# A written-out order of work, searched anew for the first stretch of a four-layer residual chain

## The chip, the cores and the metric

The kernel runs on one core of a Trainium2 chip. The metric is device time in microseconds (us) of one execution, as the median of the runs. Five engines take part, each with its own queue of instructions that it works off strictly in order: TensorE (PE, with its weight loads shown apart as PEld), VectorE (DVE), ScalarE (ACT), GpSimd (POOL) and SyncE (SP), which here does nothing but start DMA transfers. POOL starts the indirect gathers. An instruction that has to wait for another engine holds up all that stand behind it on its own engine.

## The reference

The input x has 128 sequences of 64 tokens with 256 features. Four layers are added to it one after the other, each steered by conditions of the sequence:

```python
x = x + _L0_cond_ref(x, cond_512, ...)   # modulated linear -> attention over 16 heads per token -> modulated linear
x = x + _L1_cond_ref(x, cond_512, ...)   # down and up projection with weights made per sequence, relu, residual
x = x + _L2_cond_ref(x, ids..., ...)     # layer norms with gathered gains, six terms joined, two-layer net, layer norm
x = x + _L3_cond_ref(x, cond_512, ...)   # per sequence: U = (mu @ W_dec + b_dec); out = x @ (U V) + bias
```

In layer 0 the weight is scaled by a style and a demodulation of each sequence (`style = s @ aff_w.T + aff_b`, `demod = rsqrt(sum((w*style)**2) + eps)`), and queries, keys and values are the same projection, so that the heads of one token attend to one another. Layer 1 makes `w_down = down_project * dg + db` and `w_up = up_project * ug + ub` for each sequence. Layer 2 gathers gains and offsets by token ids and adds three conditions, each of which is a small net with a layer norm of its own (`mem`, `noi`, `res`). Layer 3 makes a matrix of rank 30 for each sequence from `W_dec`.

## The kernel before, in words

The 8192 tokens are worked on in 16 blocks of 512 tokens (8 sequences). A prologue, called block -1, makes what depends on the sequences alone:

- `prologue_keys`: style and demodulation of layer 0. `style` (product on PE by `product`, L629, addition on DVE, L725), `square` on POOL (L734, L735), `root` (DVE L742, ACT L743), the copy of the demodulation of block 0 (`dmk`, ACT L767).
- `prologue_rest`: the products for layer 1 (`down_gb`, `up_gamma`, `up_beta`; copies on ACT at L790 and L795, stores to DRAM by SP at L791 and L799), the scaled weights of layer 2 (ACT L819, POOL L824 and L825), and U of layer 3. For U, 16 loads of `W_dec` (`wd`, SP L842) feed 16 groups of products (PE L851); the first eight results are moved by DVE (L866), the others by ACT (L858), and U goes to DRAM (SP L881). Then tables by rows (`by_row`, ACT L658 and L676, DVE L662 and L687, the copy ACT L901), and the three small nets (PE L629, DVE L931, ACT L937, DVE L940, DVE L958, POOL L619 and L621, DVE L964, PE L976, ACT L982, DVE L1002).

Each block then runs through `attention` and `rest`:

- loads: `xT` (SP L1039), `ids` (L1044), `dmk` (L1052), `gdb` (L1062), `wup` and `ubb` (L1073), `uT` (L1084); POOL makes `xsT` (L1097), gathers `pw` (L1112) and makes the weights of layer 1 from `gdb` (`wdn`, L1129 and L1135) and from `wup` and `ubb` (L1142, L1143).
- two pairs of attention: keys (PE L1191, DVE L1202, POOL L1213), transposes (DVE L1228, L1245), `kR` (ACT L1237), `v` (PE L1256, ACT L1261), scores (PE L1276, 128 small matmuls), their maxima (DVE L1289, ACT L1302, PE L1311, ACT L1321, DVE L1328 and L1337), the subtraction of the maxima (PE L1350), exponentials (ACT L1364, twice a pair), weighted values (PE L1381, 128 small matmuls), then DVE L1394, L1402, POOL L1405 (`att`), PE L1418, DVE L1425; after both pairs the output projection (PE L1155, DVE L1162 and L1173).
- layers 1 to 3: PE L1573, ACT L1582, PE L1591, DVE L1604, PE L1648, ACT L1655, layer norms, the eight products L1738 per half, and so on to the output store.

PSUM is shared out as four buffers `bank` and one `sc`; scores and exponentials have only the one `sc`, `kR`, `kT`, `xsT` and `gdb` exist once, `wdn` and `wup` twice. Such a buffer is a slot: who takes it next waits for its last user.

What sets the order is written out by hand: `TURNS` holds, for the prologue and each block, one number for each operation. An operation's number is `max(blk, 0) * TURN + tables[blk][k]`, and `Plan.order` emits, of all operations whose inputs are emitted and for which a slot is free, the one with the lowest number. The instructions of an engine stand in the order of emission, and the slots are given out in that order too. Blocks overlap: while block 0 is in `rest`, blocks 1 and 2 are in `attention`. `spin` is an unread product: a matmul of zeros into a `bank` that nobody reads (PE L638). Their count follows from the table of block -1:

```python
SPINS = len(TURNS[-1].split()) if -1 in TURNS else 331
...
    while plan.noted[-1] + 1 < SPINS:
        spin()
    done = plan.order()
```

## Time and profile before

| | |
|---|---|
| runs | 839.22, 828.07, 828.92, 830.99 us; median 829.96 us |
| the profiled execution | 827.48 us, of which span 825.6 us |
| granted TensorE clock, mean | 0.974 |
| VectorE, ScalarE, GpSimd | busy 588.0, 361.3, 565.2 us |
| PE busy by stretches of 10 us, 0 to 130 us | 6.33, 8.95, 7.42, 7.12, 8.85, 6.82, 5.25, 7.50, 9.09, 7.57, 8.85, 9.10, 7.83 |
| granted clock in the same stretches | 0.89, 0.93, 1.00, 1.00, 0.83, 1.00, 0.63, 0.84, 0.85, 0.83, 1.00, 1.00, 1.00 |
| DMA share in the same stretches | 0.75, 0.86, 0.62, 0.81, 0.99, 0.67, 0.90, 0.39, 0.67, 0.72, 0.44, 0.40, 0.38 |

Times in the trace count from the first instruction. "Idle before" is the time for which an engine had nothing running ahead of an instruction, with what ended it; "issue" means that nothing the profile shows held the engine. The clock is the share of full speed that PE was granted. The DMA share is the mean busy share of the core's 16 DMA engines. Queue q1 carries SP's transfers, q0 the gathers, and the queues called "instruction" carry the engines' own instructions.

### The profile page before, as it was taken

What the parts mean: (1) busy time and instruction counts of PE and PEld (TensorE: products, weight loads), DVE (VectorE), ACT (ScalarE), POOL (GpSimd) and SP (SyncE); (2) the same over time, 40 slices, a digit from 0 to 9 for tenths busy, and PEclk for the clock granted to TensorE, in tenths of its full rate; (3) what the DMA queues carried; (4) which work ended last, traced back from release to release, by engine and by line L of the source; (5) the groups of instructions that cost most, each with busy time, mean ns of one, the idle gap of its engine ahead of it and who ended that gap; (6) DMA issues with size and microseconds to landing.
All of it is one profiled execution on the core that took longest, in us unless ns stands there. A gap on an engine that the chain in (4) does not pass through costs nothing.

```text
span 825.6 us, 29444 instructions
## 1 busy us (share of the span) xinstructions
PE 755.5 (92%) x12843; PEld 489.9 (59%) x12843; DVE 588.0 (71%) x1320; ACT 361.3 (44%) x664; POOL 565.2 (68%) x544
## 2 busy tenths in 40 slices
PE   7777889999999999999999999999999989998695
PEld 5655665665666565666666666656566565654353
DVE  4646796966868686969687786869695967765435
ACT  1564335442536362544435353636254343434331
POOL 5453879394877878586869688786789485818243
PEclk9996999999999999999999999999999999999888
DMA  8786643234342234343333333342434231022001
GB/s 271 243 244 189 206 135 81 77 104 105 95 126 70 84 96 129 92 116 94 105 103 94 117 96 102 97 120 68 129 92 117 73 89 51 11 58 81 35 1 52
DMA packets 59297, 87.63 MB, mean 106 GB/s; under 512 B 6456, under 2 KB 42400, under 8 KB 59168
## 3 DMA queue, kind: packets, MB, share of 16 engines
q1 hardware_dynamic: 54048, 68.96, 28.4%
q0 software_dynamic: 5120, 16.78, 7.2%
q8 instruction: 101, 1.65, 0.9%
q14 instruction: 28, 0.23, 0.1%
HBM read 72.48 MB, written 13.24 MB: 104 GB/s over the span
## 4 chain that ended last, share of the span: by engine, by line
PE 62%; DVE 20%; issue 5%; ACT 4%; POOL 4%; DMA 3%; SPq 0%; another core or an unknown queue 0%; DVEq 0%; POOLq 0%; ACTq 0%
PE bank L1738 26%; PE bank L1785 5%; PE bank L1191 5%; PE sc L1276 4%; DVE st L611 4%; DVE mr L1289 3%; PE bank L1688 3%; PE bank L1381 2%; PE bank L1573 2%; PE bank L1155 2%; PE bank L629 2%; DVE bank L1162 2%; ACT e L1364 1%; PE bank L1648 1%; PE bank L1823 1%
## 5 line engine op out<-in xcount | busy, mean ns | idle before, releaser
L1289 DVE TENSOR_REDUCE mr<-sc 128x16 f32<-128x1024 f32 x64 | 75.7, 1210 | 16.1 <-PE sc L1276 16.1
L1364 ACT ACTIVATE e<-sc 128x1024 f32<-128x1024 f32 x64 | 62.4, 1027 | 34.3 <-PE sc L1350 34.2
L1112 POOL DMA_INDIRECT pw<-in_pw,idx x64 | 65.3, 1021 | 15.9 <-issue 8.2
L1155 PE MATMUL bank<-osT,wo 128*128 128x512 f32 x128 | 62.2, 614 | 5.2 <-DVE osT L1425 5.1
L1276 PEld LDWEIGHTS sc<-kR,kT 20*64 20x64 f32 x4096 | 48.8, 134 | 24.8 <-issue 10.9
L1738 PE MATMUL bank<-uu,w_s 128*128 128x512 f32 x128 | 63.3, 598 | 0.0
L1191 PE MATMUL bank<-wk,xsT 128*128 128x256 f32 x256 | 62.3, 386 | 1.0 <-DVE uu L866 0.6
L1738 PE MATMUL bank<-uu,w_h 128*128 128x512 f32 x128 | 62.8, 613 | 0.0
L1276 PE MATMUL sc<-kR,kT 20*64 20x64 f32 x4096 | 54.3, 236 | 8.7 <-issue 5.9
L1237 ACT ACTIVATE kR<-kT,early 128x1024 f32<-128x1024 f32 x32 | 39.7, 1241 | 51.5 <-DVE kT L1228 51.5
L1738 PE MATMUL bank<-uu,w_t 128*128 128x512 f32 x128 | 61.3, 605 | 0.2 <-ACT uu L1655 0.2
L1738 PE MATMUL bank<-x2T,w_x 128*128 128x512 f32 x128 | 60.0, 593 | 0.0
L1381 PEld LDWEIGHTS bank<-e,v 64*32 64x32 f32 x4096 | 44.3, 106 | 24.1 <-issue 20.1
L1785 PE MATMUL bank<-w,uu 128*128 128x256 f32 x240 | 55.9, 386 | 2.3 <-DVE uu L1758 2.3
L1191 PEld LDWEIGHTS bank<-wk,xsT 128*128 128x128 f32 x256 | 48.5, 196 | 12.8 <-issue 3.5
L1381 PE MATMUL bank<-e,v 64*32 64x64 f32 x4096 | 50.7, 228 | 5.5 <-issue 5.5
L1693 ACT COPY uu<-bank 128x512 f32<-128x512 f32 x64 | 36.4, 587 | 38.1 <-PE bank L1688 36.5
L1202 DVE TENSOR_TENSOR kxe<-bank,dmk 128x512 f32<-128x512 f32 x32 | 22.0, 688 | 43.5 <-PE bank L1191 38.2
L1129 POOL TENSOR_TENSOR wdn<-gdb,late 128x512 f32<-128x512 f32 x32 | 40.6, 1284 | 15.8 <-PE bank L1573 15.2
L1785 PEld LDWEIGHTS bank<-w,uu 128*128 128x128 f32 x240 | 44.4, 190 | 9.8 <-DVE uu L1758 4.1
L1228 DVE STREAM_TRANSPOSE kT<-kxe 128x512 f32<-128x512 f32 x64 | 42.1, 684 | 9.3 <-POOL kxe L1213 9.3
L1213 POOL TENSOR_TENSOR kxe<-kxe,kbr 128x512 f32<-128x512 f32 x32 | 40.7, 1273 | 10.3 <-DVE kxe L1202 10.1
(241 smaller groups left out, 1782.6 us busy)
## 6 DMA issues: line engine op xcount, KB each, us to landing
xT<-in_xT SPq DMA_DIRECT2D x32, 256.0 KB
gdb<-dgdb SPq DMA_DIRECT2D x16, 512.0 KB
ubb<-ugub SPq DMA_DIRECT2D x32, 256.0 KB
wup<-ugub SPq DMA_DIRECT2D x32, 256.0 KB
ids<-in_ids SPq DMA_DIRECT2D x16, 256.0 KB
ud<-uu SPq DMA_DIRECT2D x8, 512.0 KB
uT<-ud SPq DMA_DIRECT2D x16, 256.0 KB
dmk<-demod_k SPq DMA_DIRECT2D x60, 64.0 KB
```

The source lines that it names most:

```text
L1112: lambda tl=tl, n=n: nc.gpsimd.indirect_dma_start(out=pw[tl // 2].t[:, tl % 2, :], out_offset=None, in_=a["pw"], in_offset=bass.IndirectOf ...
L1129: lambda w=w, dp=dp: nc.gpsimd.tensor_tensor(w(), gdb.t[:, :, 0:64], dp, ALU.mult),
L1155: nc.tensor.matmul(ps.t, owT[:, c, bass.ts(oc, 128)], osT.t[:, c, :], start=(c == 0), stop=(c == C - 1))
L1191: nc.tensor.matmul(ps.t[:, bass.ts(l, F)], xsT.t[:, c, mine2].rearrange("p (n l) -> p l n", l=2)[:, l, :], kwT[:, c, :], start=(c == 0), s ...
L1213: lambda: nc.gpsimd.tensor_tensor(kxe.t[:, :, :, 0:D], kxe.t[:, :, :, 0:D], heads(kinds["kbr"][0]).unsqueeze(1).to_broadcast([128, 2, H, D ...
L1228: lambda l=l: nc.vector.transpose(kT.t[:, l, :].rearrange("p (g h t) -> p h g t", h=H, t=QT), kxe.t[:, l, :, :]),
L1276: nc.tensor.matmul(sc.t[64 * c : 64 * c + 64, q, bass.ts(tg, 64)], cut(kT.t)[r, tg // 4, c, tg % 4, :], cut(kR.t)[r, tg // 4, c, tg % 4, : ...
L1289: lambda two=two: nc.vector.tensor_reduce(mr.t[:, two, :], sc.t[:, two, :].rearrange("p q (g n) -> p q g n", g=TG), AX.X, ALU.max),
L1364: lambda k=k: nc.scalar.activation(es[k].t, sc.t[:, 2 * k : 2 * k + 2, :], AF.Exp, scale=0.25),
L1381: nc.tensor.matmul(placed(pr[c].t)[32 * q : 32 * q + 32, l, g, :, :], v.t[r, l, :].rearrange("p (g q d) -> p g q d", g=4, q=4)[:, g, q, :] ...
L1738: lambda ps=ps, w=w, src=src, fc=fc, c=c, n=n: nc.tensor.matmul(ps.t, w.t[:, c, bass.ts(fc, 128)], src.t[:, c, :], start=(n == 0 and c == ...
L1785: nc.tensor.matmul(ps.t[:, bass.ts(l, F)], s2.t[:, c, bass.ts(2 * p + l, 128)], w2.t[:, c, :], start=(c == 0), stop=(c == C - 1),)
```

## The change

Only numbers in `TURNS` change: 200 of the entries for the prologue (which grow from 254 to 260, so that there are 29 unread products rather than 23), 160 of 184 for block 0 and 186 of 188 for block 1. No operation, shape or tile is altered. The tables of blocks 2 to 15 stay.

```diff
 TURNS = {
     -1: """
-    -652225 -652207 -501809 -501797 549383 103302 97834 98988 -85347 -290328 36942 -280951 36928 -327022 -327038
...
-    15405911 16048186 16073369 -309973 14522440 16005249
+    -652225 -652207 -501809 79623 549383 100856 97834 98988 -135716 -290328 -135684 -290340 -135703 -327038 -327044
...
     """,
     0: """
-    -484581 84372 -652203 -35682 684863 1289506 1005368 578863 1258365 2419509 2111364 2061858 1597541 357479
...
+    -484581 84372 -652203 -135703 684863 1289506 1005368 1030611 944977 2419509 2111364 2063037 1598720 357479
...
     """,
     1: """
-    -394079 -394092 -482733 -425615 -297831 -337865 -325537 -299039 -482716 297196 735637 407985 -421370 1532404
...
+    -475790 -480517 -480506 -439237 -295604 -295623 -306545 -306564 -481411 409304 726230 398578 374496 1282148
...
     """,
```

The numbers mean something only through the order that follows from them. On each engine that order is the old one but for moves over a few places, all within about the first 220 us. Those of the first 110 us that pass more than a neighbour, or pass one of another kind:

| engine | what moves |
|---|---|
| SP | load of `idx` behind `w2` and the first half of block 0's `xT` |
| SP | both halves of block 1's `xT` ahead of a `wd`, `down_gb` and `up_gamma` |
| SP | the four `dmk` loads of block 1 ahead of the store L791 |
| SP | second `ubb` load of block 0 ahead of two `wd`, `int_b1` and `mem_W1` |
| SP | `ids` and `gdb` of block 2 ahead of the `wup` loads of block 1 |
| PE | second `dmk` product (L629) ahead of a style product and of the first keys of block 0 (L1191) |
| PE | first keys of block 1 (L1191) behind the second scores of block 0 (L1276) |
| PE | of the two `wd` products (L851) after that, the later one first |
| PE | L1311 of block 0's second pair ahead of a `wd` product (L851) |
| PE | second transposes of block 0 (L1648) ahead of block 1's second L1381 |
| ACT | `v` of block 0 (L1261) ahead of `kR` (L1237) and three others |
| ACT | L1302 of block 0's second pair ahead of an L858 and an L819; the three L819 still ahead of L1321 |
| ACT | `kR` of block 1 (L1237) and an L858 ahead of the exponentials of block 0's second pair (L1364) |
| ACT | L1655 of block 0 ahead of two L982 |
| DVE | maxima (L1289) of block 0's second pair ahead of block 1's L1202; of block 1's first pair ahead of two L1228 |
| POOL | `xsT` of block 1 (two L1097) behind L1213 and a gather of block 0 |
| POOL | L1142 of block 1 behind two L1129 of block 2 and the L1143 of block 0 that follows them |

Of the unread products seven stand at the start as before, one moves from 119 us to ahead of the first L1311 near 33 us, two are put in near 150 to 160 us and two near 655 us, near 725 us there are two fewer, and at the end of the last block four more.

## The prediction

> **What bounds the kernel now.** I read the page first (busy times, slices), then the chain of waits, then the PE timeline of the first 130 us, because the change orders only what runs there. The page says that TensorE (PE) is the bound, and where it is not:
>
> ```profile
> PE 755.5 (92%) x12843; PEld 489.9 (59%) x12843; DVE 588.0 (71%) x1320; ACT 361.3 (44%) x664; POOL 565.2 (68%) x544
> ...
> PE   7777889999999999999999999999999989998695
> ...
> q8 instruction: 101, 1.65, 0.9%
> ```
>
> A slice is 20.6 us: PE is at 7 to 8 tenths in the first six and at 9 after that. By stretches of 10 us it is busy 100.7 of the first 130 us and 42.74 of the 44 us from 200 to 244. What this change can win or lose lies in those 29 us; later delays pass to the end, since PE has no slack to take them up. The largest pieces, from the PE timeline (start, duration, line, what it writes and reads, count, idle time before and who ended it):
>
> ```profile
> 37.31 1.90 PE L1191 MATMUL bank<-wk,xsT 128*128 128x256 f32 x8
> 40.30 1.59 PE L1276 MATMUL sc<-kR,kT 20*64 20x64 f32 x128 [1.09 <-ACT kR L1237]
> ...
> 45.88 1.62 PE L1381 MATMUL bank<-e,v 64*32 64x64 f32 x128
> ...
> 50.48 0.66 PE L1418 MATMUL bank<-ident,att 128*128 128x128 f32 x4 [1.33 <-POOL att L1405]
> ...
> 56.38 1.42 PE L1381 MATMUL bank<-e,v 64*32 64x64 f32 x121
> 61.31 0.31 PE L1381 MATMUL bank<-e,v 64*32 64x64 f32 x7 [3.51 <-issue]
> 61.55 0.49 PE L629 MATMUL bank<-early,p 128*128 128x128 f32 x2
> 61.97 1.92 PE L1276 MATMUL sc<-kR,kT 20*64 20x64 f32 x119
> 67.33 0.49 PE L1276 MATMUL sc<-kR,kT 20*64 20x64 f32 x9 [3.44 <-issue]
> 67.75 1.12 PE L1256 MATMUL bank<-ident,kV 128*128 128x128 f32 x4
> ```
>
> Two stops of 3.51 and 3.44 us stand inside a run of equal matmuls, with nothing that PE waits for ("issue"). Between them lie 7+2+119 = 128 matmuls, with their weight loads 256 instructions; queue q8 moved 1.65 MB in 101 packets, 16.3 KB each. So these are instruction blocks that came late. Stretches of 1 us show why (PE, PEld, DVE, ACT, POOL busy, clock, DMA share, GB/s):
>
> ```profile
> 57.00:58.00 1.00, 0.80 (x84) 0.65 (x66) 0.23 (x1) 0.74 (x4) 0.83 (x1) 1.00 0.68 242
> 58.00:59.00 1.00, 0.00 (x0) 0.00 (x0) 0.53 (x2) 0.77 (x2) 0.00 (x0) 1.00 0.20 67
> 59.00:60.00 1.00, 0.00 (x0) 0.00 (x0) 0.57 (x2) 0.89 (x4) 0.00 (x0) 1.00 0.00 0
> ...
> 64.00:65.00 1.00, 0.00 (x0) 0.00 (x0) 0.37 (x2) 0.85 (x2) 0.00 (x0) 0.50 1.17 241
> ```
>
> In the trace's packets q8's block starts at 58.92, when the last data packet is through, takes 0.97 us, and PE goes on at 61.31, 2.4 us after the start. The next block starts at 64.52, 3.2 us after the resumption, amid a burst of loads, and PE goes on 2.8 us later. After the stops the granted clock is 0.50 from 62.5 to 72.7.
>
> [...]
>
> **The change part by part.** I read the new order out of the tables by the rule of `order()`: the lowest number among operations whose inputs and slots are ready. PE's sequence changes little: the same 7 early unread products, then swaps of neighbours. The order of each engine is the old one from about 220 us on, and so are nearly all slots' predecessors. Both late block boundaries stay where they were, one matmul earlier in L1381 and in L1276. So the fetches are not removed; what moves is when PE and the DMA queue reach them.
>
> (1) *Start, to 31 us.* On SP xT of block 1 goes ahead of a `wd`, `down_gb` and `up_gamma`; it no longer stands behind the `wd` slot wait at 18.73 and issues near 14.6. On PE L629 for the second half of `dmk` goes ahead of the keys; the keys come 1.1 us later, behind ACT L767. Cover: DVE's L1245 at 20.67 waits on the `wd` landing at 18.76 and L866 anyway. The two `demod_o` products swap while DVE keeps its order: the scores come 0.3 late, taken up by the 0.62 us fetch stop at 26.80. I take 0; without cover +1.1.
>
> (2) *Keys of block 1 behind the second scores.* L1191 at 37.31 now runs after L1276, so PE idles from 37.4 to 40.3 (L1276 still waits for ACT L1237, behind both exps), and the 1.90 us fall into a stretch with no gap until 49.15. One unread product ahead of L1311 adds 0.22 (119.03 to 119.25, start to start). L1381 at 45.88 comes 2.1 later.
>
> (3) *ACT.* PE now feeds the two `wd` products (L851, 42.68) in reversed order while ACT takes the old first one first: its L858 starts at 48.0 rather than 44.63. Behind it: 1.26, the copies L1302 0.49, the other L858 1.26, three L819 at 0.72: L1321 at 53.1 rather than 49.37. Behind that, L1237 (1.24) and an L858 (1.26) now precede the exps: 57.0 rather than 53.31. L1381 (56.38) starts near 59.8, +3.5, and would reach the block's end at 61.2.
>
> (4) *The first fetch.* It ran when the DMA queue was empty. SP's issues before it hang on L799, which waits for ACT L795 behind PE's L629 at 41.83 (now +1.9), and on freed `wd` slots: I shift them 1.0 to 1.5, so the fetch starts at 60.2 and PE resumes at 62.6: +1.3; 2.2 of the 3.5 fall into time lost anyway. Bounds: 0 (queue unmoved) and +3.5 (moves with the work).
>
> (5) *The second fetch.* PE reaches it 2.58 after the resumption, at 65.2. The burst that delayed it is released by ACT L901, 59.44 before and 61.6 now. Asked ahead of the burst, the block starts 1.3 after the resumption (as it did at 28.74 after the stop that ended at 27.42) and PE goes on at 66.7; in it, 3.2 and 68.6. I take 67.6: +0.3 against 67.33; with both ends of (4), -1.9 to +2.2.
>
> (6) *Clock.* In the half-clock stretch L1256 takes 1.12 (0.66 elsewhere), L1418 1.06 (0.66), twelve L851 2.77 (1.59 by 1.06 for eight): 2.0 lost. Shorter stops may free a third of it: -0.7 (0 to -2.0; above 0 if the gap of (2) halves the clock too).
>
> [...]
>
> (7) *POOL.* L1142 of block 1 ran at 71.44, inside an idle time of 10.61 us ahead of L1129. It now follows L1143 at 85.77, ahead of L1097 (88.42), att and ry, which the chain of waits runs through: +1.25 (0 to 1.27).
>
> (8) *ACT's L1655 ahead of two L982.* PE's L629 at 95.66 waited 1.43 for the bank that DVE L1202 frees; it now gets the bank of L1655, free by 93.6. The next gate is L982, 95.07: -1.0. DVE is full from 110 to 120 (9.25 of 10), so half stays: -0.5 (0 to -1.9).
>
> (9) *Six more unread products*, 0.22 each where PE is full: +0.5 (0 to 1.3). Swaps among neighbours elsewhere: 0, bounds -0.7 to +0.7 (one DVE row of 0.68).
>
> Sum of (5), which contains (2) to (4), and (6) to (9): +0.3-0.7+1.25-0.5+0.5 = +0.85 on the profiled execution's 827.48 us (span 825.6): 828.3. The runs are 828.07, 828.92, 830.99 and 839.22, median 829.96; the lower three average 829.3. I forecast **830.0 us: no difference**.
>
> **Rivals.** *Slower by over 1%:* the loads move with the work, so both stops remain whole behind the 3.5 us of (3); the gap of (2) halves the clock for two more stretches of 3.4 us (1.7 each); (7) and (9) are paid, (8) is not: 3.5+3.4+1.3+1.3 = +9.5, 838 to 839. It decides from where the first late block starts after 61.5. For: every link is a wait in the profile. Against: most of SP's issues there wait for nothing. *Faster by over 1%:* both blocks are asked for in a free queue: -3.5-3.4-2.0 = -8.9, 821. Against: PE has only 2.58 us between the boundaries, and even the free case costs 1.3+2.8. *Smaller gain:* the second block precedes the burst and the clock stays whole: about -4, 826. *Smaller loss:* (4) at its upper end: +5, 834. *The change does not do what it says:* later-asked fetches cost the same, the rest cancels; this lies inside the forecast.
>
> **How the numbers follow.** A measurement of this kernel can tell about 1%, 8.3 us. Chances: forecast (827 to 832.5) 0.45, smaller loss 0.23, smaller gain 0.17, slower by over 1% 0.11, faster by over 1% 0.04. Leaving out a tenth on either side: 823 to 838.
>
> **What would show it.** Right: the stops in L1381 and L1276 still there, the first under 2 us and ended near 62.6; PE idle over 2.5 us before L1276 at 40; L1142 between L1143 and L1135 near 87; L629 with no wait near 95. Wrong: a first stop of 3 us or more, new "issue" stops of over 1 us, or half-clock stretches after 100 us that before does not have.

## The result and the profile after

The changed kernel is slower, by less than one per cent. Before has a median of 832.89 us (69 runs, 823.59 to 843.12), after of 837.62 us (43 runs, 830.92 to 845.05); the ratio is **1.0070 [1.0054, 1.0086]**, that is about 5.8 us. Runs over 1.5% above the fastest of their kernel are left out of all ratios and of the means and differences below. The forecast was no difference, 830.0 us, on a median of before of 829.96 (its first four runs). The 837.62 us lie inside the range of 823 to 838 and within the 1% that was set as the bound, but the kernel did move, and the rival that came nearest was the "smaller loss" (834), for another reason than the one given for it.

The profiled execution of after took 838.04 us (span 836.3, mean clock 0.968), that of before 827.48 (825.6, 0.974). They lie 10.6 us apart and the kernels 5.8: each profile is one draw from its kernel's spread. Which of the 10.6 us belong to the change had to be found by runs.

From the page of after (busy times; the span in 40 slices of 20.9 us; the instruction queue):

```profile
PE 763.6 (91%) x12849; PEld 494.4 (59%) x12849; DVE 592.2 (71%) x1320; ACT 361.1 (43%) x664; POOL 566.2 (68%) x544
...
PE   7677888999999999999999999999999979998696
...
PEclk8989999999999999999999999999999989999888
...
q8 instruction: 101, 1.65, 0.9%
```

The picture is that of before: 7 to 8 tenths in the first slices, 9 after that, the same 1.65 MB of instructions in 101 packets. Three things differ. The second PE slice has 6 tenths. The clock is lower in the first slice and in the third (42 to 63 us), and higher in the fourth (63 to 84 us; 9 tenths, 6 in before). The slice from 669 to 690 us has 7 tenths and a lower clock.

The PE timeline of after for the stretch that the prediction worked out (start, duration, line, what it writes and reads, count, idle time before and what ended it):

```profile
37.02 1.16 PE L851 MATMUL bank<-early,wd 128*128 128x128 f32 x8
43.48 2.27 PE L1276 MATMUL sc<-kR,kT 20*64 20x64 f32 x128 [5.30 <-ACT kR L1237]
45.67 3.78 PE L1191 MATMUL bank<-wk,xsT 128*128 128x256 f32 x8
...
52.65 1.49 PE L1381 MATMUL bank<-e,v 64*32 64x64 f32 x128
...
64.10 1.55 PE L1381 MATMUL bank<-e,v 64*32 64x64 f32 x128
...
66.00 1.51 PE L1276 MATMUL sc<-kR,kT 20*64 20x64 f32 x119
69.17 0.35 PE L1276 MATMUL sc<-kR,kT 20*64 20x64 f32 x9 [1.66 <-issue]
```

The second scores (L1276) start at 43.48, not at 40.30, after 5.30 us with nothing to do; they and the keys behind them (L1191) then run at half clock (0.50 granted from 42.53 to 49.36), 2.27 and 3.78 us in place of 1.59 and 1.90. The weighted values (L1381) start 6.8 us late, at 52.65. But of the two stops of before, 3.51 and 3.44 us, the first is gone (128 matmuls of L1381 in one piece) and the second is 1.66 us. So the delay of 6.8 us has shrunk to 69.17 - 67.33 = 1.8 where the second stop ends.

Below, "late" at a time t means: the median, over PE's operations that before's profile starts near t, of their start in one profile less their start in before's profile. After is 6.7 us late at 44 us, 1.3 at 75, 0.3 at 104, 3.1 at 132, 3.9 at 640, 8.8 at 700 and 10.5 at 735. Four pieces ask for an explanation: what happened at 40 us, what between 104 and 132, what near 670, and the last 1.7 us, a stretch at half clock from 735 to 739 in after's profile that before's lacks.

### The profile page after: what moved, and what is told of

The parts are those of the page before. It is cut to its first block, busy times and chain, and to the rows that moved or that the text cites. A ratio compares the mean times of both kernels' runs of the same rounds, so it can differ in the third digit from the quotient of the medians.

```text
span 836.3 us, 29459 instructions
## 1 busy us (share of the span) xinstructions
PE 763.6 (91%) x12849; PEld 494.4 (59%) x12849; DVE 592.2 (71%) x1320; ACT 361.1 (43%) x664; POOL 566.2 (68%) x544
## 3 DMA queue, kind: packets, MB, share of 16 engines
q8 instruction: 101, 1.65, 0.9%
## 4 chain that ended last, share of the span: by engine, by line
PE 63%; DVE 21%; ACT 5%; POOL 5%; issue 4%; DMA 1%; SPq 0%; DVEq 0%; POOLq 0%; ACTq 0%
PE bank L1738 25%; PE bank L1191 6%; PE bank L1785 5%; DVE mr L1289 4%; PE sc L1276 4%; DVE st L611 4%; PE bank L1688 3%; PE bank L1381 3%; DVE bank L1162 2%; PE bank L1573 2%; PE bank L629 2%; ACT e L1364 2%; PE bank L1648 1%; PE bank L1823 1%; PE bank L1591 1%
## 5 line engine op out<-in xcount | busy, mean ns | idle before, releaser
L1289 DVE TENSOR_REDUCE mr<-sc 128x16 f32<-128x1024 f32 x64 | 75.6, 1211 | 13.6 <-PE sc L1276 13.6
L1112 POOL DMA_INDIRECT pw<-in_pw,idx x64 | 65.4, 1021 | 15.8 <-issue 7.9
L1364 ACT ACTIVATE e<-sc 128x1024 f32<-128x1024 f32 x64 | 62.3, 1026 | 30.5 <-PE sc L1350 30.4
L1191 PE MATMUL bank<-wk,xsT 128*128 128x256 f32 x256 | 67.6, 410 | 2.4 <-POOL xsT L1097 1.0
L1213 POOL TENSOR_TENSOR kxe<-kxe,kbr 128x512 f32<-128x512 f32 x32 | 41.0, 1280 | 35.3 <-DVE kxe L1202 35.1
L1276 PEld LDWEIGHTS sc<-kR,kT 20*64 20x64 f32 x4096 | 48.4, 132 | 27.4 <-issue 9.0
L1237 ACT ACTIVATE kR<-kT,early 128x1024 f32<-128x1024 f32 x32 | 39.8, 1243 | 55.9 <-DVE kT L1228 55.9
L1276 PE MATMUL sc<-kR,kT 20*64 20x64 f32 x4096 | 53.6, 235 | 10.9 <-ACT kR L1237 5.3
L1191 PEld LDWEIGHTS bank<-wk,xsT 128*128 128x128 f32 x256 | 51.6, 209 | 16.3 <-issue 4.4
L1381 PEld LDWEIGHTS bank<-e,v 64*32 64x32 f32 x4096 | 44.5, 106 | 24.3 <-issue 18.5
L1381 PE MATMUL bank<-e,v 64*32 64x64 f32 x4096 | 51.2, 228 | 6.9 <-issue 5.1
L1202 DVE TENSOR_TENSOR kxe<-bank,dmk 128x512 f32<-128x512 f32 x32 | 22.0, 687 | 47.8 <-PE bank L1191 44.7
L1228 DVE STREAM_TRANSPOSE kT<-kxe 128x512 f32<-128x512 f32 x64 | 42.2, 685 | 10.2 <-POOL kxe L1213 9.5
L1129 POOL TENSOR_TENSOR wdn<-gdb,late 128x512 f32<-128x512 f32 x32 | 40.7, 1281 | 12.6 <-PE bank L1573 12.5
```

The costliest lines, as they stand in the source:

```text
L1112: lambda tl=tl, n=n: nc.gpsimd.indirect_dma_start(out=pw[tl // 2].t[:, tl % 2, :], out_offset=None, in_=a["pw"], in_offset=bass.IndirectOf ...
L1129: lambda w=w, dp=dp: nc.gpsimd.tensor_tensor(w(), gdb.t[:, :, 0:64], dp, ALU.mult),
L1191: nc.tensor.matmul(ps.t[:, bass.ts(l, F)], xsT.t[:, c, mine2].rearrange("p (n l) -> p l n", l=2)[:, l, :], kwT[:, c, :], start=(c == 0), s ...
L1213: lambda: nc.gpsimd.tensor_tensor(kxe.t[:, :, :, 0:D], kxe.t[:, :, :, 0:D], heads(kinds["kbr"][0]).unsqueeze(1).to_broadcast([128, 2, H, D ...
L1228: lambda l=l: nc.vector.transpose(kT.t[:, l, :].rearrange("p (g h t) -> p h g t", h=H, t=QT), kxe.t[:, l, :, :]),
L1276: nc.tensor.matmul(sc.t[64 * c : 64 * c + 64, q, bass.ts(tg, 64)], cut(kT.t)[r, tg // 4, c, tg % 4, :], cut(kR.t)[r, tg // 4, c, tg % 4, : ...
```

## The experiments

Each kernel was timed in five rounds against before on the same chip. The chips differ from run to run (before's median was 833.12 us on one and 824.06 on another), so a kernel is told by its ratio to before; two kernels are compared directly only where the text says that they shared a chip. All of them compute the whole reference.

### Where the wait at 40 us comes from

POOL in after (same columns; the number in brackets is the idle time before):

```profile
34.57 1.27 POOL L1213 TENSOR_TENSOR kxe<-kxe,kbr 128x512 f32<-128x512 f32 x1 [10.06 <-DVE kxe L1202]
35.99 0.99 POOL L1112 DMA_INDIRECT pw<-in_pw,idx  x1
36.99 2.05 POOL L1097 TENSOR_TENSOR xsT<-xT,style_k 128x512 f32<-128x512 f32 x2
38.99 1.26 POOL L1129 TENSOR_TENSOR wdn<-gdb,late 128x512 f32<-128x512 f32 x1
40.33 1.26 POOL L1135 TENSOR_TENSOR wdn<-wdn,gdb 128x512 f32<-128x512 f32 x1
```

DVE in after, where the line of interest is the first:

```profile
36.53 3.76 DVE L810 TENSOR_SCALAR wsm<-wsm 128x6 f32<-128x6 f32 x1
40.20 0.70 DVE L1245 STREAM_TRANSPOSE kV<-kxe 128x512 f32<-128x512 f32 x1
40.83 1.25 DVE L1228 STREAM_TRANSPOSE kT<-kxe 128x512 f32<-128x512 f32 x2
```

DVE in before:

```profile
35.75 0.45 DVE L810 TENSOR_SCALAR wsm<-wsm 128x6 f32<-128x6 f32 x1
36.20 0.71 DVE L1245 STREAM_TRANSPOSE kV<-kxe 128x512 f32<-128x512 f32 x1
```

POOL in before:

```profile
34.90 1.27 POOL L1213 TENSOR_TENSOR kxe<-kxe,kbr 128x512 f32<-128x512 f32 x1
36.32 0.99 POOL L1112 DMA_INDIRECT pw<-in_pw,idx  x1
```

L810 multiplies 128 x 6 numbers. It takes 3.76 us in after, and the row shows it as busy, not as idle: no wait names it. It ends at 40.29, and POOL, which has worked from 36.99 without a pause, makes its first one from 40.25 to 40.33. In before L810 starts inside POOL's L1213 and ends at 36.20, just behind that instruction's end at 36.17; there it lasts 0.45 us. All sixteen profiles in which DVE runs L810 show the same: it ends 0.03 to 0.04 us after the end of a POOL instruction, whatever its length. So in these traces L810 waits while POOL works and gets through in a gap of POOL's stream, in after one of 0.08 us; below this is called the hold. It does not touch every DVE instruction: the transpose L1245 behind it takes its usual 0.70 us beside POOL's L1135. What the change did was to move POOL's two L1097 from ahead of L1213 to behind the gather L1112, which closes the gap that follows L1112 in before (37.31 to 37.73, a wait for `gdb`); and L810 itself comes 0.78 us later, when POOL has already passed its pause between L1213 and L1112. Behind L810 on DVE stand the transposes L1245 and L1228, behind those ACT's `kR` (L1237), and behind that the scores for which PE waits.

In after L810 was held through the rest of the gather and three more POOL instructions in a row (2.05 us for two L1097, 1.26 for L1129) and released only where the stream had a gap. What in the chip makes the hold, no run shows.

Two runs test it from both sides. In both, the keys of block 1 (PE L1191), which read what L1097 writes, change place with the second scores along with it. **pool_back** is after with before's numbers for the two L1097 (table of block 1):

```diff
-    1193293 1161391 1209564 -129480 -147706 1078814 1094978 444778 1813295 177455 -504031 213695 -504015 806623
+    1193293 1161391 1209564 -1264679 -1264697 1078814 1094978 444778 1813295 177455 -504031 213695 -504015 806623
```

> The changed kernel with POOL's two L1097 of block 1 ahead of L1213 again, as before, and with it L1191 of block 1 ahead of the second scores. In the changed kernel DVE's L810, 128x6, takes 3.76 us from 36.53 (0.45 before) while POOL runs L1112, L1097 twice and L1129 with no gap, and the scores start 3.2 us late. [...] The 6 us do not reach the end: a late instruction block stops PE again near 60, PE is within 1 us of the changed kernel at 104, and the time is within 1.5 us of it. Rival (the late front is a part of the loss): the time falls by 2 us or more. Other rival (L810 waited for something other than POOL): it still takes over 2 us.

The 6 us are those of L1381: it started at 52.65 in after, and this run was to bring it to 46 or 47. Measured: 1.0050 [1.0017, 1.0083]; L810 takes 0.23 us, again at the end of POOL's L1213 (DVE, then POOL), and the profile is 2.0 us early at 104 us.

```profile
39.21 0.23 DVE L810 TENSOR_SCALAR wsm<-wsm 128x6 f32<-128x6 f32 x1
```

```profile
38.14 1.27 POOL L1213 TENSOR_TENSOR kxe<-kxe,kbr 128x512 f32<-128x512 f32 x1
```

**pool_only** is before with after's two numbers:

```diff
-    443756 1548772 1282128 -1264679 -1264697 916581 1275890 1398962 1806910 176525 220234 -35053 255915 516626
+    443756 1548772 1282128 -129480 -147706 916581 1275890 1398962 1806910 176525 220234 -35053 255915 516626
```

> The kernel before with POOL's two L1097 of block 1 behind L1213 and the gather L1112, as in the changed kernel, and with it the keys L1191 of block 1 behind the second scores. Theory: L810 takes 2.5 to 3.8 us instead of 0.45, the second scores start 2 to 4 us later and PE's L1381 near 46 by 4 to 6; none of it reaches the end, since the late instruction blocks near 60 have come by then: 0.999 to 1.001 of the kernel before. [...]

Measured: **1.0111 [1.0075, 1.0146]**, the slowest of all, from two numbers. Its DVE and then its POOL:

```profile
37.83 7.62 DVE L810 TENSOR_SCALAR wsm<-wsm 128x6 f32<-128x6 f32 x1
```

```profile
37.50 0.99 POOL L1112 DMA_INDIRECT pw<-in_pw,idx  x1
38.51 2.04 POOL L1097 TENSOR_TENSOR xsT<-xT,style_k 128x512 f32<-128x512 f32 x2
40.51 2.47 POOL L1129 TENSOR_TENSOR wdn<-gdb,late 128x512 f32<-128x512 f32 x2
42.95 2.47 POOL L1135 TENSOR_TENSOR wdn<-wdn,gdb 128x512 f32<-128x512 f32 x2
```

Here `wdn` is made in pairs with no pause between them, and L810 is held through the rest of the gather and all six instructions behind it, to 45.45; POOL's last one ends at 45.42. PE waits 9.08 us for `kR`, and the profile is 8.0 us late at 104 us.

The third test keeps every order and takes L810 off VectorE: ScalarE makes the product.

```diff
-        dve(6, lambda: nc.vector.tensor_scalar(w(0, 6), w(0, 6), w(7, 8), None, ALU.mult), [wsm], [wsm])
+        act(6, lambda: nc.scalar.activation(w(0, 6), w(0, 6), AF.Identity, scale=w(7, 8)), [wsm], [wsm], table=0)
```

**pool_act** has this edit on pool_only, **after_act** on after, and **after_again** is after unchanged, on the same chip.

> The kernel before with POOL's order alone changed (1.011 of the kernel before), and the multiplication L810, 128x6, done by ACT instead of DVE; nothing else moves. Theory (the 7.6 us for which L810 held DVE are the loss): no DVE instruction of that stretch takes over 1.4 us, the second scores start before 43.5, and the time falls to 0.998 to 1.003 of the kernel before. Rival (the order of POOL and of the keys costs by itself): 1.007 or more.

> The changed kernel with L810 done by ACT. Theory: the second scores start 2 to 3 us sooner after the first L1311 than in the changed kernel (9.67 us after it there), no half clock in them, and the time falls by 2 to 4 us against the changed kernel on the same chip, to 1.002 to 1.004 of the kernel before. Rival (the late instruction blocks take the gain): within 0.15% of the changed kernel.

> The changed kernel once more, unchanged. All theories: 1.005 to 1.009 of the kernel before, L810 at 2.5 to 3.8 us, the scores after it at half clock (2.27 us). The profile says for one more execution whether the stop near 674 and a half-clock stretch between 110 and 140 us come; both came in most of the kernels with the new order, each in some only.

Measured: pool_act 1.0011 [0.9973, 1.0050], from 1.0111 (on another chip): the one per cent was the hold, and without it the new place of L1097, and of the keys with it, costs nothing that the interval can tell. ACT makes the product in 0.30 us, beside POOL's gather L1112. After_again 1.0097 [1.0059, 1.0134], after_act 1.0049 [1.0007, 1.0092]. Compared directly, drawing the twelve and eleven times anew many times, the ratio of the means of after_again to after_act lies between 1.0007 and 1.0077 in 95 of 100 draws; the means are 3.4 us apart (833.3 and 829.9). PE in after_act:

```profile
40.16 1.59 PE L1276 MATMUL sc<-kR,kT 20*64 20x64 f32 x128 [2.82 <-ACT kR L1237]
41.69 3.65 PE L1191 MATMUL bank<-wk,xsT 128*128 128x256 f32 x8
...
48.53 1.48 PE L1381 MATMUL bank<-e,v 64*32 64x64 f32 x128
```

The wait before the scores is 2.82 us, the "over 2.5" of the prediction, and the scores start at 40.16, where the prediction had left them. The remaining lateness of L1381 (48.53 against 45.88) is the term of the prediction's step 2, 2.1 us, with half-clock keys on top.

### Which half of the new order costs the rest

**front_new** takes after's numbers for all that ran before about 100 us and before's numbers for the rest (255 numbers differ from after); **front_old** is the reverse (258 differ from before). Below, the new front is the new order up to about 100 us, the old front that of before. The first line of the table of block -1 in front_old, as an edit of after, shows the kind of edit:

```diff
-    -652225 -652207 -501809 79623 549383 100856 97834 98988 -135716 -290328 -135684 -290340 -135703 -327038 -327044
+    -652225 -652207 -501809 -501797 549383 103302 97834 98988 -85347 -290328 36942 -280951 36928 -327022 -327038
...
```

> The new order on every engine up to 100 us, with its eight unread products, and the old order after it, with the sixteen others of before. Theory (the lasting loss is made between 100 and 130 us): PE is within 1.5 us of the kernel before at 100 and stays so at 130 and 650; the time is 1.000 to 1.002 of the kernel before. Rival (the front makes the loss: L810 behind POOL, the keys behind the scores, the half clock): 4 to 5 us late at 130, 1.005 to 1.006.

> The reverse: the old order and its seven unread products up to 100 us, and the new order after it with the twenty-one others. Theory: PE level with the kernel before at 100, 3 to 5 us late at 130 and 650; 1.004 to 1.006 of the kernel before. Rival: level at 130, 1.000 to 1.002.

Measured: front_new 1.0020 [0.9985, 1.0056], front_old 1.0003 [0.9973, 1.0032]. Neither half alone shows a loss that can be told from none. In front_new L810 takes 2.55 us, so the hold is in it in a shorter form. **front_act** is front_new with L810 on ScalarE:

> The new order up to 100 us and the old one after it, with L810 done by ACT. Theory: 0.997 to 1.001 of the kernel before, below the same order with L810 on DVE (1.002). Rival: 1.002 or more, so that the start or the swap of keys and scores costs too.

Measured: 1.0007 [0.9971, 1.0043]; its profile is 3.7 us early at 104 us. After_act ran on the same chip, and the two differ only in the order after about 100 us and in the five more unread products that after_act has there (at 0.22 us each, 1.1 us at most). The means, 829.9 and 825.2 us, are 4.7 us apart, and drawn anew as above their ratio lies between 1.0019 and 1.0095. So, **on the new front, the new order after 100 us costs**, apart from the hold. The means of after_again (833.3), after_act (829.9) and front_act (825.2), with before at 825.3 on that chip, go from after back to before in two steps, and the rest of the new front costs nothing that these runs can tell.

Most of it shows between 104 and 132 us. In the ten profiles with the new order there, PE loses 2.8 to 7.2 us in that stretch against before's profile, mean 5.08 (after itself 2.75); in the ten with the old order, before among them, it loses 0 to 3.3, mean 1.44: 3.6 us between the two groups, and 4.6 if the stretch is drawn out to 640 us. PE of after in that stretch:

```profile
122.17 0.30 PE L1381 MATMUL bank<-e,v 64*32 64x64 f32 x2
124.20 1.63 PE L1381 MATMUL bank<-e,v 64*32 64x64 f32 x126 [1.74 <-DVE x2T L1604]
125.76 0.66 PE L1256 MATMUL bank<-ident,kV 128*128 128x128 f32 x4
127.21 0.66 PE L1648 MATMUL bank<-ident,x2T 128*128 128x128 f32 x4 [0.80 <-DVE x2T L1604]
```

L1381 has to wait for a bank that DVE's L1604 frees. In before DVE runs one L1604 ahead of the pair of L1289 (118.97 and 119.54); in after the pair comes first (121.22, 2.34 us) and L1604 at 123.47. That invites putting it back. **mlp_back** and **mlp_only** exchange the numbers of the `res` net's L931 and L940, the nearest other move on DVE; **dve_back** does the same as mlp_back and puts back L1604 and L1425 of block 1 as well:

```diff
-    2093369 1298624 1477279 1950442 1950438 1404270 2200384 1402214 1923896 1744276 1286021 1463895 2326105 1885484
-    2326100 1334102 1339036 1395441 2306717 2306701 2434583 2225829 2261725 2543401 2525610 1755644 1736339 2579505
+    2093369 1298624 1477279 1950442 1950438 1404270 2200384 1402214 1923896 1744276 1286021 1463895 2192488 1885484
+    2159446 1334102 1339036 1395441 2306717 2306701 2434583 2225829 2261725 2543401 2525610 1755644 1736339 2579505
...
-    736860 505315 -391412 778275 736839 334400 334398 1026582 1139175 1139194 404535 1078835 1032561 1154323 1032521
-    1290732 1295890 573437 1294685 1295900 1018378 1399025 1018360 1518562 1486103 1508613 1630513 2142794 1691142
+    736860 505315 -391412 778275 736839 334400 334398 1026582 1139175 1139194 404535 1078835 1032561 1171507 1032521
+    1290732 1295890 573437 1294685 1295900 1018378 1399025 1018360 1518562 1472691 1508613 1630513 2142794 1691142
```

The first four lines are mlp_back, all of them dve_back; mlp_only puts after's 2326105 and 2326100 into before.

> The changed kernel with one thing undone: DVE's L931 and L940 of one small MLP run again before L1245 of block 2 and L1002, not behind them; PE's L629 that reads them goes back ahead of L1591. Theory (this is the lasting loss): in the changed kernel L1381 stops 1.74 us on L1604 at 122 us and PE is 3.0 us late at 130; here L1276 comes back to about 117.4, the stop inside L1381 is under 0.5 us, PE is at most 1 us late at 130 against the kernel before, and the time falls by about 3 us, to 1.003 of the kernel before. Rival (the loss is made elsewhere, in late instruction fetches): the stop goes, the time stays within 1 us of the changed kernel's, 1.007.

> The kernel before with that one thing alone: DVE's L931 and L940 behind L1245 of block 2 and L1002. Theory: L1276 near 117.4 comes about 1 us later, L1381 behind it waits over 1 us for L1604 or another freed bank, PE is 2 to 3 us late from 130 on, 1.003 to 1.004 of the kernel before. Rival: within 1 us, 1.000 to 1.001.

> The changed kernel with three DVE swaps undone: L1289 of block 2 ahead of L1425 of block 1 again (in the changed kernel DVE stands idle from 105.08 to 106.86 for PE's L1418 with the scores ready), L931 and L940 ahead of L1245 and L1002, and the first L1604 ahead of both L1289. Theory (DVE, full from 105 to 125, hands each wait on): the first L1289 starts within 1.5 us after its scores, the stop inside L1381 at 122 is under 0.4 us, PE gains 2.5 to 4 us between 105 and 130 on the changed kernel; 1.002 to 1.004 of the kernel before. Rival (these swaps are worth under 1 us together): 1.006 to 1.008.

Measured: mlp_back 1.0085 [1.0053, 1.0118], mlp_only 0.9984 [0.9949, 1.0019], dve_back 1.0054 [1.0024, 1.0083]. None of these moves carries the loss. Why undoing the L1604 wait brought nothing that can be told is in dve_back's PE timeline:

```profile
124.25 0.67 PE L1381 MATMUL bank<-e,v 64*32 64x64 f32 x43
127.11 1.14 PE L1381 MATMUL bank<-e,v 64*32 64x64 f32 x85 [2.18 <-issue]
128.17 1.11 PE L1256 MATMUL bank<-ident,kV 128*128 128x128 f32 x4
129.62 1.11 PE L1648 MATMUL bank<-ident,x2T 128*128 128x128 f32 x4 [0.34 <-DVE x2T L1604]
```

L1381 now starts without a wait, gets 43 matmuls far, and stops for 2.18 us with "issue", as at the late instruction blocks near 60 us. After_again waits 1.74 us for L1604 ahead of its third matmul there and stops for only 0.18 us at the same 43rd; in after the instruction block of that stretch starts at 122.04 and is through at 123.37, before the wait of 1.74 us ends at 124.20. So the wait had covered that fetch. Old-order profiles have the same stop at the same place (mlp_only 1.64, front_new 1.64, front_act 1.52 us), without the half clock behind it, but for best_new (1.92 us, with it): in dve_back L1256 and L1648 take 1.11 us in place of 0.66. A stretch at half clock between 110 and 140 us is in eight of the ten profiles with the new order and in one of ten with the old. Stretches of 10 us of after_again (PE, PEld, DVE, ACT, POOL busy, clock, DMA share, GB/s):

```profile
110.00:120.00 10.00, 8.09 (x48) 4.50 (x48) 9.15 (x15) 2.74 (x6) 4.26 (x4) 0.83 0.47 142
120.00:130.00 10.00, 7.92 (x317) 6.27 (x316) 7.24 (x19) 3.92 (x8) 7.34 (x8) 1.00 0.47 107
130.00:140.00 10.00, 8.00 (x93) 6.11 (x81) 7.01 (x12) 7.08 (x14) 9.30 (x10) 0.83 0.09 28
```

The clock is 0.83 in the first and the third, 1.00 in all three in before. But a half-clock stretch of 3.41 us (before's at 42.0 is one) costs 1.7 us at most, an estimate from its length, and after's own profile has none between 110 and 140 us and loses 2.75 us there, so the clock is only a part. There is no single long stop ahead of it, but several short waits in a row (L976 0.65, L629 0.90 us near 115; L1381 1.74 near 128). Which of the moves after 100 us brings the short waits together was not separated. One measurement stands against a simple sum: front_old has the whole new order after 100 us on the old front, its own profile loses 2.8 us from 104 to 132, and yet its ratio allows 0.32% (2.7 us) at most. That the order after 100 us needs the new front's arrival times to cost its full 4.7 us is possible, and not shown.

### The start

The change puts the second `dmk` product (PE L629) ahead of the first keys of block 0. **start_back** is after with a number that puts it back behind them (table of block -1):

```diff
-    -331362 -35713 99192 -35708 76051 -500885 -331376 318100 -327069 315689 -539809 -293298 228511 -327040 434975
+    -331362 -35713 99192 -35708 76051 -500885 -331376 318100 -320110 315689 -539809 -293298 228511 -327040 434975
```

> The changed kernel with one thing undone at the start: PE's L629 for the second half of dmk behind the keys L1191 of block 0 again. In the six profiled executions with the new start these keys take 3.4 to 3.6 us, in the four with the old one 1.90, and PE is 0.7 to 3.5 us late at 30 us, 2.3 in the mean. Theory (the start is the larger part of what the front loses): the keys take about 1.9 us, start about 1 us sooner, PE is 1.5 to 2.5 us earlier at 30 than that mean, and 1 to 2 us of it reach the end: 1.004 to 1.006 of the kernel before. Rival (later waits take it up): 1.006 to 1.008.

Measured: 1.0073 [1.0043, 1.0104]. The time did not move. In its profile PE is 0.3 us early at 30 us (after: 0.8 late, pool_back 3.4, front_new 3.5), but so it is in after_act, and front_act is 0.8 early, both with the new start: these keys take 3.1 to 3.6 us in six of the eleven profiles with it and 1.90 in the other five. So one profile cannot tell what the edit did at 30 us. At 104 us start_back is 0.6 late and after 0.3: what is lost at the start is taken up before that.

### The stop near 670 us

PE of after there:

```profile
673.29 1.45 PE L1381 MATMUL bank<-e,v 64*32 64x64 f32 x124
678.95 0.42 PE L1381 MATMUL bank<-e,v 64*32 64x64 f32 x4 [4.20 <-issue]
679.30 2.93 PE L1191 MATMUL bank<-wk,xsT 128*128 128x256 f32 x6
```

PE of before at the same work:

```profile
669.38 1.45 PE L1381 MATMUL bank<-e,v 64*32 64x64 f32 x125
671.73 0.30 PE L1381 MATMUL bank<-e,v 64*32 64x64 f32 x3 [0.89 <-issue]
671.95 2.00 PE L1191 MATMUL bank<-wk,xsT 128*128 128x256 f32 x8
```

4.20 against 0.89 us, with the keys at half clock behind the longer one: 4.9 us of lateness in one step. The orders are the same in both kernels here. In the trace's packets an instruction block is asked for at that time, and SP's load of `xT`, 2.78 us before the last L1591 ends in before, after and after_again, is cut into packets of 2 KB. In before the block starts 2.11 us before that end, ahead of most of the data, and the one after it 1.38 us behind the end. In after it starts 1.47 us before the end, just when the data packets are through (the last starts 1.43 before), and the next block only 4.71 us behind it, after a burst of 1 KB packets. All twenty profiles divide in this way: the block starts 1.4 to 1.8 us before that end in the seven with a long stop, and 2.1 to 2.9 in the thirteen without. Two runs give the load that makes those 1 KB packets, `wup` of block 15 (SP), a later place, about 1.1 us behind the end of the last L1591 rather than 0.04; two others put in ten more unread products, five of them ahead of that stretch and five after it:

```diff
-    -4648505 -1156507 -4635552 -163816 -4614966 -3735477 -4773557 -3708250 -4656482 -4559710 -4572079 187994
+    -4648505 -1156507 -4635552 -163816 -4614966 -3735477 -4773557 -3708250 -4656482 -122500 -4572079 187994
```

is **load_after** on after and **load_before** on before;

```diff
-    -302053 15394192 16034132 14522442 -331757 16046838 16046865 3098908 3226051 11288552 14520045 16046827 16037492
+    -302053 15394192 16034132 14522442 -331757 16046838 16046865 3098908 3226051 11288552 14520045 16046827 16037492
+    11068225 11068225 12073260 12073260 12073260 12929925 12929925 12929925 12929925 12929925
```

is **tie_after**, and the same ten numbers at the end of before's table of block -1 are **tie_before**.

> The changed kernel with SP's load L1071 of block 15 behind L1084 of block 13 instead of ahead of it, so that its 1 KB packets start some 0.6 us later. In the changed kernel's profile an instruction block that was due at 673.06 went behind these packets and PE stopped 4.20 us at 674.75; in the profile of before it went 0.06 us ahead of them and PE stopped 0.89. Theory (a tie that the changed kernel loses in most executions): no stop over 1.2 us near 674, and the time falls by 3 to 5 us, to 1.001 to 1.003 of the kernel before. Rival (that execution was a chance): the time stays within 1 us of the changed kernel's.

> The kernel before with SP's load L1071 of block 15 behind L1084 of block 13. Theory (a tie near 670 us that the kernel before loses in about half of its executions, for 5 us; its times lie in two groups, near 830 and near 835): the group near 835 empties and the median falls by 2 to 4 us, to 0.995 to 0.998 of the kernel before. Rival (the two groups are made elsewhere, as at the front): both groups stay, within 0.2% of the kernel before.

> The changed kernel with ten more unread products between 567 and 667 us, where PE waits anyway (2 ahead of L1155, 3 ahead of L1688 at 621, 5 in the wait of 0.95 us ahead of L1688 at 667). Every later block boundary falls ten matmuls earlier, near 668 some 0.35 us. In ten profiled executions the block that PE needs at 672 starts 2.1 to 2.9 us before the end of the last L1591 there in the six without the long stop, and 1.4 to 1.6 in the four with it; the packets of a load of xT start 2.78 us before it in all ten: a tie. Theory: asked for 0.35 us sooner the block always goes first, no stop over 1.5 us near 674, and the median falls by 3 to 4 us, to 1.002 to 1.004 of the kernel before. Rival (the outcome hangs on something else): the long stop comes as often, the time stays within 1 us or rises by what the products cost.

> The kernel before with the same ten unread products in the same waits. Theory: its executions lose that tie less often, so there is less to win: no stop over 1.5 us near 670, the median falls by 0.5 to 2 us, 0.997 to 1.000 of the kernel before. Rival: within 0.1%, or slower by the cost of the products, up to 1 us.

Measured: load_after 1.0043 [1.0007, 1.0080], load_before 0.9983 [0.9954, 1.0012], tie_after 1.0066 [1.0038, 1.0094], tie_before 0.9977 [0.9949, 1.0004]. Each interval overlaps that of the kernel from which it was made. In load_after's profile the stop is 0.26 us, in tie_before's 0.81. Over all profiles the long stop (3.1 to 4.2 us) is in after, mlp_back, dve_back, front_new, pool_only, pool_act and after_act, and a short one (0.3 to 1.2 us) in before, after_again and the others. It is in four of the ten profiles with the new order after 100 us and in three of the ten with the old one, and after_again is the same kernel as after. So it is a matter of the execution, worth about 5 us to one, and makes half of the gap between the two profiles; that it makes the difference of the kernels, nothing here shows. Whether it makes the spread of each kernel is open. With the ten products the twelve runs of tie_before lie between 819.84 and 825.27, while before's 34 on that chip reach 834.48 and eleven of them are above 826; but best_old below, with the same products, reaches 828.82. Nor did it happen as meant. The five products ahead of that end delay PE by 0.86 us and not the load, so its packets start 3.64 us before that end and not 2.78, and tie_after gained nothing.

### Putting together what helped

**best_old** is before with the ten products and the load of load_before; **best_new** is front_act with the same two edits.

> The kernel before with the ten unread products in PE's waits between 567 and 667 us and SP's load L1071 of block 15 behind L1084. Theory (a late instruction block near 670 us makes the slower half of the executions): no stop over 1.5 us near 670, no execution over 2% above the fastest, median 0.995 to 0.998 of the kernel before. Rival: 0.998 to 1.001.

> The same ten products and the same load order in the kernel with the new order up to 100 us, L810 done by ACT, and the old order after. [...] Other rival (start and swap still cost): above best_old by 0.3% or more.

Measured: best_old 0.9981 [0.9953, 1.0010], best_new 0.9996 [0.9969, 1.0023]. Neither beats before beyond its interval, and the new front without the hold is no better than the old one. The nearest to a gain is tie_before, 0.9977 [0.9949, 1.0004].

## Why the prediction was wrong, step by step

**The bound and the place.** Right: the time moved in the first 130 us. The gain or loss was to be looked for in the 29 us that PE idles there, and both causes lie in it.

**(1) Start, 0.** Nothing speaks against it. PE was between 0.8 us early and 3.5 late at 30 us in profiles with the new start, up to more than the 1.1 given as the uncovered price; start_back, which undoes one of its moves, did not move the time.

**(2) Keys behind the scores: the step that failed.** It let PE idle "from 37.4 to 40.3" and took the scores' start at 40.30 as given, since "L1276 still waits for ACT L1237, behind both exps". ACT's L1237 has a second input, the transposes on DVE, and DVE was held by POOL. The measured idle time runs from 38.2 to 43.48, and L1381 came 6.8 us late rather than 2.1. The cause is an edit that got no price at all: POOL's two L1097 behind L1213 and a gather. The table of moves lists it; the working costed of POOL's moves only L1142. Its measured price is 3.4 us by the means of after_again and after_act on one chip (0.6 to 6.4 by the interval above), 4.0 by their two ratios to before; in the profiles at 104 us the eight with the new front and the hold (after and after_again among them) are 3.1 us later (mean +0.9) than the four with the new front without it (mean -2.2). No row of before could show 3.76 us, but one could show that the hold exists: L810 at 0.45 us, ending 0.03 us after L1213 does.

**(3) ACT.** The size was off with (2): L1321 ran at 57.16 for a predicted 53.1, and the second L1381 at 64.10 for 59.8. The step's +3.5 sat on a start that was 4 us too early.

**(4) The first fetch, resumed at 62.6.** It did not stop at all. The block started at 63.18 (58.92 in before, 60.2 in the forecast), 4.26 us later than in before, and PE began that L1381 at 64.10, 7.72 later than in before: it came to the boundary so late that the block was there. The sign of the argument (a fetch that moves by less than the work does costs less) was right, and it hid most of the hold: 6.7 us late at 44, 1.3 at 75. Stops of this kind also vary from one execution to the next: in profiles with the old front the two are 0.58 and 1.38 (mlp_only), 0.92 and 1.93 (front_old), 2.45 and 3.57 (load_before), 2.99 and 3.37 (best_old).

**(5) The second fetch.** Resumed at 69.17, +1.8 against 67.33; forecast +0.3, bounds -1.9 to +2.2. Inside the bounds, near their upper end. That end was itself too low: with (4) at +3.5 and the block in the burst, the step's own numbers give 70.8, +3.5, as the rival "slower by over 1%" has it.

**(6) Clock, -0.7.** Right on the stretch it spoke of, and outweighed by its own proviso, "above 0 if the gap of (2) halves the clock too". After in stretches of 10 us:

```profile
40.00:50.00 10.00, 5.98 (x136) 4.61 (x136) 4.95 (x7) 2.88 (x6) 4.01 (x4) 0.66 0.77 258
...
60.00:70.00 10.00, 7.84 (x281) 5.36 (x280) 6.15 (x12) 6.29 (x15) 5.24 (x5) 0.99 0.53 168
```

The clock is 0.99 between 60 and 70 (0.63 in before) and 0.66 between 40 and 50 (0.83). The 5.30 us without work were paid for once more in the 2.27 and 3.78 us behind them. Shorter waits stand ahead of half clock too: after_act's keys at 41.69 run at it (3.65 us) behind a wait of 2.82 us, and the stretches after 100 us have waits of 0.65 to 1.74 us ahead of them. The -0.7 itself, a third of the 2.0 us lost in before, was the author's estimate; no run prices it alone.

**(7) L1142 later.** As predicted in place, and within the bounds in price. POOL of after:

```profile
87.34 1.26 POOL L1142 TENSOR_TENSOR wup<-wup,late 128x512 f32<-128x512 f32 x1
```

PE's second part of the keys (L1191, waiting for POOL's L1097) starts at 92.08, 1.57 after its 90.51 in before; the stretch began about 0.9 late, so some 0.65 are left for this step, half of the forecast +1.25.

**(8) L1655 earlier.** The wait of 1.43 us ahead of L629 is gone, as predicted, and it gained nothing. After's PE:

```profile
95.72 0.48 PE L629 MATMUL bank<-p 64*128 64x128 f32 x2
96.69 1.67 PE L629 MATMUL bank<-p,p 128*128 128x256 f32 x4 [0.48 <-ACT p L982]
98.15 1.06 PE L1648 MATMUL bank<-ident,x2T 128*128 128x128 f32 x4
99.14 1.93 PE L1381 MATMUL bank<-e,v 64*32 64x64 f32 x128
```

L629 starts at 95.72, 0.06 later than before, because the products ahead of it came later; L982 is the next gate, as named, with 0.48 us; and L1648 is now ahead of L1381, so that L1381 starts at 99.14 rather than 97.57.

**(9) Unread products and neighbours.** No run prices the products alone. "Swaps among neighbours elsewhere: 0, bounds -0.7 to +0.7" is the second step that failed: the order after 100 us costs 4.7 us between after_act and front_act, of which five products can make 1.1. The prediction priced that stretch by the length of one DVE row. Its list of what would show it wrong names half-clock stretches after 100 us that before does not have, and most profiles of the new order have one; how the swaps bring the waits and these stretches about stays open.

**The sum.** By the profiles: the hold 3.1, the order after 100 us 5.08 - 1.44 = 3.6, and -0.8 for the rest of the new front (mean -2.2 at 104 us without the hold, -1.4 in the six with the old front): 5.9 us, against 5.8 measured; with the 4.6 us that the two groups are apart at 640 us it is 6.9, so the close agreement is luck. By the means on one chip: 3.4 + 4.7 - 0.1 = 8.0 from after_again over after_act and front_act to before. Both say that the hold and the order after 100 us carry the loss; how it divides between them is known to a few microseconds only, and front_old (1.0003) speaks against a fixed price of the second. The rival "smaller loss" gave +5, but by the fetch of step 4 at its upper end, and that fetch in fact won time.

## What to carry to other kernels

Before moving work on GpSimd, look at what VectorE runs beside it: a small VectorE instruction that shows as busy for microseconds may be held, as L810 was (3.76 us in after, 0.45 in before); no wait in the profile named it, and it ended 0.03 to 0.04 us after a GpSimd instruction did. Price a reordering by every engine's moves, the idle-looking ones too, and ask of each wait you take as fixed whether its second input still comes in time. When one wait goes, look for the fetch or transfer that it had covered: here 1.74 us of waiting for L1604 in after came back as 2.18 us of "issue" in dve_back.

## What the runs showed of the hardware

- A VectorE `tensor_scalar` of 128 x 6 numbers in SBUF took 0.23 to 0.45 us behind the rest of one POOL instruction, and 2.54, 3.76 and 7.62 us where POOL's instructions followed each other without a gap; in all sixteen profiles it ended 0.03 to 0.04 us after a POOL instruction did. A gap of 0.08 us was enough to let it through (after, 40.25 to 40.33). The same work on ScalarE took 0.30 us in pool_act, beside POOL's gather.
- Near 670 us PE stopped for 3.1 to 4.2 us in the seven profiles in which an instruction block started 1.4 to 1.8 us before the end of the last L1591, and for 0.3 to 1.2 us in the thirteen in which it started 2.1 to 2.9 us before it; in after, with the half clock behind it, this is about 5 us of a run of 830. It happens in some executions of a kernel and not in others (after, after_again).
- Short waits can be followed by half clock: so were 0.65 and 0.90 us around one product near 115 us in after_again, while single stops of 1.64 us (mlp_only, near 121) and 1.52 us (front_act, near 119) were not. In after's own profile two waits of 1.74 and 0.80 us near 125 were not either, so it differs from execution to execution. In each of the twenty profiles the half-clock stretches start a whole number of 3.41 us apart (in before at 7.9, 42.0, 62.5, 79.6 and 96.6 us, in after at 8.4, 15.2, 42.5, 69.8 and 97.1). Whether the place of a wait between these instants matters, no run tests.
